# A two-layer graph attention kernel: the sums placed one superchunk behind the links, the merge two behind, the edge features one ahead, with fewer small VectorE instructions

## The chip, the cores and the metric

The kernel runs on one core of one Trainium2 chip. The metric is the device time of one execution in microseconds. Three runs of the kernel before gave 5592.37, 5597.21 and 5601.2 us; the median is 5597.21 us.

Five engines and the DMA queues work side by side, each through its own list of instructions in order, and they wait for each other through semaphores. TensorE (PE) multiplies matrices into PSUM, VectorE (DVE) and ScalarE (ACT) work on tiles in SBUF and PSUM, GpSimd (POOL) here issues the gathers, and SyncE (SP) issues the plain DMAs.

## What is computed

Two graph attention layers over N = 6250 nodes with 256 features and E = 200000 edges that are sorted by destination. Every node also has a loop edge to itself, whose features are the mean over its incoming edges. The outer call is `x + two_layers(relu(layernorm(x)))`. One layer is, with the setup left out:

```python
te = relu(edge_attr @ We + be) * exp(x @ Wo + bo)[src][:, None]
s2, d2, ea2 = _add_self_loops(src, dst, te, n)
hx = (x @ Wg).reshape(n, h, f)
he = (ea2 @ Wge).reshape(-1, h, f)
al = leaky_relu(einsum('nhf,hf->nh', hx, a_s)[s2] + einsum('nhf,hf->nh', hx, a_d)[d2]
                + einsum('ehf,hf->eh', he, a_e), 0.2)
m = segment_max(al, d2, num_segments=n)
al = exp(al - m[d2])
al = al / segment_sum(al, d2, num_segments=n)[d2]
out = segment_sum(hx[s2] * al[:, :, None], d2, num_segments=n) + b
```

Layer 0 has 4 heads of 64 features and a relu behind its residual, layer 1 has one head of 256. All data is float32.

## The kernel before

A prologue makes the table T of layer 0: for each node a row of transformed features and small per-node terms. The edges of a layer are cut into 1563 chunks of 128 edges, one edge to a partition, and the chunks into 66 superchunks: 64 of 24 chunks, then one of 14 and one of 13. A step of the main loop (`edges`) works on one superchunk `st`; the names `nx`, `pv` and `pp` mean the superchunk after it, the one before it and the one before that. The two layers make 132 steps. The instructions are written out by hand in the order in which each engine runs them.

What belongs to one superchunk, with the lines that the profile names:

- `gather` (L769): 24 indirect DMAs on POOL's queue, 128 rows of T each, into one of three buffers G. The gather of superchunk k needs the buffer of superchunk k - 3, so it waits until that one's sums are done. It is issued a step ahead, at the start of the step of k - 1; the sums that it waits for run in the step before that one.
- `nodes` (L823, L825): SP's loads of the destination window's rows (tw). `load_ea`, `load_lb` and `load_fl` load edge attributes, positions and flags for two superchunks at a time.
- `spread` (L859, L861), `parts` (L881 to L893; L890 is a matmul into the PSUM tile zad), `rphase1` (matmuls L842 into y, ACT copies L843 into R), `rphase2` (L851, from R into zad), `adst` (matmuls L907 into zad, transposes L909, a reduction L911): the edge features and the destination's term, as a row for each edge.
- `logits` (L922 to L936, DVE): the attention logits and two scans that give running maxima of each destination's edges within a partition's line of chunks.
- `ends` (L947, L948, PE transposes; L950, ACT): the ends of these lines, turned so that the 128 partitions lie in one row, are copied from the PSUM tile lf into LF.
- `links` (L962 to L969, DVE; L974, PE): two scans over LF and the flags chain the partitions' maxima, and transposes bring the result back into a tile named lf. That PSUM tile has one buffer.
- `maxima` (L984 to L1006): the maxima of each edge's destination, the weights exp(al - m) in kps and the factor pr for what is carried over from the superchunk before.
- `onehots` (L871): the selection matrices S that say which edge belongs to which row of the window.
- `scale` (L1032): the gathered rows in G times their weights, in pieces of 6 chunks.
- `carried` (L1017 to L1023): the row that the superchunk before left open (carry) is added into the first row of G.
- `sums` (L1044): S times G, one product per chunk, all 24 into one PSUM tile u; then ACT copies u to U (L1047). A product of float32 shows as two matmul records. `carry` (L1053, L1055) takes the open row from U.
- `merge` and what follows (L1065 to L1119 in layer 0, to L1145 in layer 1), here called `finish`: the loop edge, the normalisation, the residual and, in layer 0, the next layer's input. `rows1` (L1125, L1127) transposes it, `rows2` multiplies it with the next layer's weights (L378), adds (L382), takes one exponential (L1135) and stores the row of T for layer 1 (L1160). In layer 1 `rows2` stores the output (L1165).

In the step of superchunk k the order is: the gather and the loads of k + 1; logits of k; carried and the first 12 sums of k - 1; spread of k + 1; ends of k; rows1 of k - 2; 6 more sums of k - 1; links and onehots of k; rows2 of k - 2; the last 6 sums of k - 1 with U; maxima of k in turn with parts of k + 1; rphase1 of k + 1; the carry of k - 1; scale of k in turn with the merge of k - 1; rphase2 and adst of k + 1. The last superchunk of a layer has a function of its own (`last`), which also starts the next layer.

Of the kernel before, what the change touches and what calls it, by code (L numbers as in the profile page):

```python
# [31 lines left out]
P = 128  # L32
# [46 lines left out]
class Kernel:  # L79
# [279 lines left out]
    def fixed_rows(self):  # L359
        nc, cp = self.nc, self.cp  # L360
        self.crow = crow = [cp.tile([1, L.W], F32, name=f"crow{L.l}") for L in self.L]
        for t in crow:
            nc.gpsimd.memset(t, 0.0)
# [190 lines left out]
    def edges(self, ctx):  # L554
# [24 lines left out]
        drain(self.parts(steps[0]))  # L579
# [4 lines left out]
        pv = pp = None  # L584
        ahead, rest = 1, None
        for k, st in enumerate(steps):

            if ahead < len(self.groups):
                left = self.groups[ahead][0] - 2 - k
                if rest is None and left <= 2:  # L590
                    gi = self.index_load(ahead, self.xp)
                    rest = self.index_group(ahead, self.xp, gi)
                if rest is not None:
                    for _ in range(7):
                        next(rest, None)
                    if left <= 0:
                        drain(rest)
                        ahead, rest = ahead + 1, None
            nx = steps[k + 1] if k + 1 < len(steps) else None
            self.load_lb(k + 2)  # L600
            if st["s"] + 1 == self.NS:
                self.last(st, pv, nx)
                pv = pp = None
                continue
            self.gather(nx)
            self.nodes(nx)
            drain(self.logits(st))
            n = pv["C"] if pv else 0
            if pv:
                self.carried(pv)  # L610
                self.sums(pv, 0, n // 2)
            self.spread(nx)
            self.ends(st)
            if pp:
                self.rows1(pp)
            if pv:
                self.sums(pv, n // 2, 3 * n // 4)
            self.links(st)
            self.load_fl(k + 1)
            if k != self.NS:  # L620
                self.onehots(st)
            if pp:
                self.rows2(pp)
            if pv:
                self.sums(pv, 3 * n // 4, n)
            weave(self.maxima(st), self.parts(nx))
            if k == self.NS:
                self.onehots(st)
            drain(self.rphase1(nx))
            self.load_ea(k + 2)  # L630
            if pv:
                self.carry(pv)
            weave(self.scale(st), self.finish(pv) if pv else ())
            self.rphase2(nx)
            self.adst(nx)
            if nx["s"] + 1 == self.NS:
                n = st["C"]
                self.carried(st)
                self.sums(st, 0, n // 2)
                if pv:  # L640
                    self.rows1(pv)
                self.sums(st, n // 2, 3 * n // 4)
                if pv:
                    self.rows2(pv)
                    pv = None
                self.sums(st, 3 * n // 4, n)
            pp, pv = pv, st
# [4 lines left out]
    def last(self, st, pv, nx):  # L652
# [27 lines left out]
        n = st["C"]  # L680
        self.sums(st, 0, n - 2)
# [6 lines left out]
        self.sums(st, n - 2, n)  # L688
# [4 lines left out]
        self.rows2(st)  # L693
        if nx:
# [4 lines left out]
            drain(self.parts(nx))  # L699
            self.rphase2(nx)  # L700
            self.adst(nx)
            if early:
                self.added(nx, [(w, self.trow1[q["s"] % 2][:, :self.L[1].TW]) for w, q in ((w0, pv), (w1, st))])
# [112 lines left out]

    def nodes(self, st):
        nc, L, s = self.nc, st["L"], st["s"]
        r = nc.sync.value_load(self.base_i[0:1, 0, s:s + 1], min_val=0, max_val=self.N)
        tw = self.np_.tile([P, self.L[0].TW + D], F32, name="tw", bufs=3)  # L820
# [53 lines left out]
    def parts(self, st):  # L874
# [7 lines left out]
        yield  # L882
        V.tensor_sub(r[:, :H], ad, a3[:, :H, 0])
        yield
        V.tensor_copy(a3[:, :H, 1], r[:, :H])
        yield
        V.tensor_sub(a3[:, :H, 2], r[:, :H], a3[:, :H, 1])
        st["zad"] = z = self.ps_1.tile([P, 1024], F32, name="zad")
        q = z[:, 400:400 + 3 * H]
        self.nc.tensor.matmul(q, st["Q"], a3[:, :H, :].rearrange("p h t -> p (h t)"), start=True, stop=True)  # L890
        yield
        st["aq"] = aq = self.aq[st["k"] % 2]
        V.tensor_tensor(aq[:, :, 4:4 + 3 * H], q.unsqueeze(1).to_broadcast([P, 4, 3 * H]),  # L893
                        self.quad.unsqueeze(2).to_broadcast([P, 4, 3 * H]), op=OP.mult)
        yield

    def adst(self, st):


        nc, L, c = self.nc, st["L"], st["C"]  # L900
        H = L.H
        V = nc.vector
        z, lb = st["zad"], st["lb"]
        st["rt"] = rt = self.wp.tile([P, C, 32], F32, name="rt", bufs=1)
        rv = rt.rearrange("p c j -> p (c j)")
        for w, o in self.halves(st):
            nc.tensor.matmul(z[:, o], st["aq"].rearrange("p k j -> p (k j)"), lb[:, w], start=False, stop=True)  # L907
        for w, o in self.halves(st):
            V.transpose(rv[:, w], z[:, o])  # L909
# [30 lines left out]
    def ends(self, st):  # L940
# [5 lines left out]
        pl = self.ps_1.tile([P, 512], F32, name="lf")  # L946
        nc.tensor.transpose(pl[0:H, 1:P + 1], fv[:, :, c - 1], self.ident)  # L947
        nc.tensor.transpose(pl[0:H, P + 1:2 * P + 1], bv[:, :, 0], self.ident)  # L948
# [3 lines left out]
    def links(self, st):  # L952
# [12 lines left out]
        st["cl"] = cl = self.wp.tile([4, 2, P], F32, name="cl")  # L965
        init = -BIG if prev is None else prev["cl"][:H, 0, P - 1:P]
        V.tensor_tensor_scan(cl[:H, 0, :], fl[:H, 1, :], d1[:H, 0, :], init, op0=OP.add, op1=OP.max)  # L967
        V.memset(cl[:H, 1, P - 1:P], -BIG)
# [4 lines left out]
        for i in range(2):  # L973
            nc.tensor.transpose(pc[:, i * H:(i + 1) * H], cl[:H, i, :], self.ident[0:H, 0:H])  # L974

    def maxima(self, st):
# [9 lines left out]
        for i, pen in enumerate((self.fpen, self.lpen)):  # L986
            V.tensor_tensor(th, pen[:, o:o + c].unsqueeze(1).to_broadcast([P, H, c]),  # L987
# [12 lines left out]
        if st["prev"] is not None:  # L1000
            st["pr"] = pr = self.wp.tile([1, 4], F32, name="pr")
            V.tensor_sub(pr[:, :H], pc[0:1, 0:H], mh[0:1, :, 0])
            yield
# [286 lines left out]
def drain(g):  # L1290
    for _ in g:
        pass
# [91 lines left out]
```

## Time and profile before

The profiled execution took 5582.45 us, 5580.7 us of which is its span, from its first instruction to its last.

| what | value |
|---|---|
| runs, median | 5597.21 us |
| profiled execution; its span | 5582.45 us; 5580.7 us |
| mean granted TensorE clock in the span | 0.756 of full speed |
| steps of layer 0: first gather starts | 199.8 us |
| steps of layer 0: last one counted starts | 2781.2 us |
| steps of layer 1: first gather counted starts | 2995.7 us |
| steps of layer 1: last one counted starts | 5487.3 us |
| one indirect DMA of a gather on POOL | 0.95 us, and 0.30 us to the next |
| one gather of 24 | 29.8 to 30.0 us |
| sums, 12 chunks (24 records) at speed; 6 chunks after idle time | 5.63 us; 4.88 us |
| scale, one piece of 6 chunks | 1.75 us |
| onehots of a superchunk | 3.32 us |

How to read the profile: busy times are per engine, in us; shares are of the span. A line of the timeline has the start in us, the duration, the engine, the line of the kernel, the instruction, its output and inputs with the shape, the number of instructions drawn together, and in brackets the idle time just before and what ended it. "remote" stands where the event that released the wait is not one that the profile can name, "issue" where the engine waited for nothing that is shown. In a windows line the window comes first, then its length, then busy time and count of PE, PEld (weight loads), DVE, ACT and POOL, the granted TensorE clock, the busy share of the DMA engines and their GB/s.

### The profile page before, as it was taken

How to read it: one execution, taken by the hardware profiler on the slowest of the kernel's cores; microseconds unless marked ns; L12 is line 12 of the kernel's file. 1: busy time of each engine (PE TensorE's matmuls, PEld its weight loads, DVE VectorE, ACT ScalarE, POOL GpSimd, SP SyncE). 2: the span in 40 equal slices, each digit the busy share in tenths (PEclk: the TensorE clock that was granted, in tenths of full speed). 3: DMA queues.
4: the chain of work that ended last, by engine and by line, in shares of the span. 5: the costliest groups of instructions: out<-in, count | busy, mean ns of one | idle time of the engine just before them, and what ended most of it. 6: DMA issues, size and time to landing. Idle time of an engine off the chain costs nothing. (4 is left out here: it accounts for less than half of the span.)

```text
span 5580.7 us, 39554 instructions
## 1 busy us (share of the span) xinstructions
PE 2861.8 (51%) x10408; PEld 1925.1 (34%) x10408; DVE 2922.8 (52%) x8141; ACT 687.9 (12%) x1910; POOL 2979.8 (53%) x3155
## 2 busy tenths in 40 slices
PE   6455455555555555555654544445444454444445
PEld 4233333333333333333443323333233232333324
DVE  6555555555555555555654544545454454544546
ACT  4111111111111111111110100101010010101001
POOL 3455555555555554555554555555555555555553
PEclk8677777777777777777777777767777777777777
DMA  6333333333333333333333333333333333333332
GB/s 198 94 102 115 104 100 111 107 98 107 109 104 104 111 104 102 108 105 105 104 106 86 101 105 99 107 101 105 104 96 108 99 107 102 99 109 94 110 100 66
DMA packets 246401, 584.96 MB, mean 105 GB/s; under 512 B 62904, under 2 KB 103310, under 8 KB 246104
## 3 DMA queue, kind: packets, MB, share of 16 engines
q0 software_dynamic: 150144, 422.82, 27.4%
q1 hardware_dynamic: 95610, 158.89, 8.8%
q8 instruction: 85, 1.39, 0.1%
q14 instruction: 146, 1.20, 0.1%
q10 hardware_dynamic: 416, 0.67, 0.0%
HBM read 547.87 MB, written 34.37 MB: 104 GB/s over the span
## 5 line engine op out<-in xcount | busy, mean ns | idle before, releaser
L769 POOL DMA_INDIRECT G<-T,src x3114 | 2963.0, 952 | 2546.6 <-issue 905.2
L1044 PE MATMUL u<-G,S 128*128 128x270 f32 (+1 forms) x6252 | 1775.2, 445 | 3.6 <-ACT pr L1006 2.4
L1044 PEld LDWEIGHTS u<-G,S 128*128 128x128 f32 x6252 | 1389.3, 226 | 311.0 <-ACT pr L1006 2.5
L964 DVE TENSOR_TENSOR d<-LF,fl 4x256 f32<-4x256 f32 (+1 forms) x132 | 54.5, 413 | 1907.8 <-ACT LF L950 1902.1
L974 PE MATMUL lf<-ident,cl 4*128 4x4 f32 (+1 forms) x264 | 64.3, 245 | 1917.5 <-DVE cl L967 1903.2
L1032 DVE TENSOR_TENSOR G<-G,kps 128x1536 f32<-128x1536 f32 (+2 forms) x528 | 907.9, 1727 | 1.2 <-ACT R L843 1.2
L974 PEld LDWEIGHTS lf<-ident,cl 4*128 4x128 f32 (+1 forms) x264 | 45.6, 174 | 1980.5 <-issue 1199.7
L842 PE MATMUL y<-ea,webd 64*128 64x384 f32 (+1 forms) x1056 | 423.3, 526 | 24.9 <-ACT R L843 20.1
L871 DVE TENSOR_TENSOR S<-kps,loc 128x3072 f32<-128x3072 f32 (+2 forms) x133 | 432.8, 3254 | 0.1
L950 ACT ACTIVATE LF<-lf 4x256 f32<-4x256 f32 (+1 forms) x132 | 49.5, 375 | 2992.4 <-remote 2819.5
L947 PE MATMUL lf<-ident,fw 128*4 128x128 f32 (+1 forms) x132 | 41.2, 312 | 568.8 <-issue 263.9
L843 ACT ACTIVATE R<-y,webd 128x384 f32<-128x384 f32 (+2 forms) x528 | 293.2, 568 | 107.0 <-PE y L842 76.1
L842 PEld LDWEIGHTS y<-ea,webd 64*128 64x128 f32 x1056 | 181.7, 193 | 267.9 <-ACT R L843 136.3
L947 PEld LDWEIGHTS lf<-ident,fw 128*4 128x4 f32 (+1 forms) x132 | 10.7, 81 | 619.3 <-issue 522.1
L851 PE MATMUL zad<-R,wea 128*64 128x384 f32 (+1 forms) x1056 | 208.9, 517 | 0.3 <-DVE aq L893 0.3
L909 DVE STREAM_TRANSPOSE rt<-zad 128x384 f32<-128x384 f32 (+1 forms) x264 | 136.0, 553 | 37.8 <-remote 32.9
L1023 DVE TENSOR_TENSOR G<-G,crow 1x270 f32<-1x270 f32 (+1 forms) x130 | 55.8, 429 | 174.6 <-remote 102.8
L378 PE MATMUL fin<-wg,h1T 128*128 128x260 f32 x264 | 134.3, 662 | 4.0 <-ACT h1T L1127 3.6
L859 DVE TENSOR_TENSOR lb<-lb,kps 128x768 bf16<-128x768 bf16 x132 | 122.0, 924 | 11.4 <-issue 11.4
L1047 ACT ACTIVATE U<-u 128x270 f32<-128x270 f32 (+1 forms) x132 | 51.9, 393 | 597.6 <-PE zad L890 534.8
L851 PEld LDWEIGHTS zad<-R,wea 128*64 128x64 f32 x1056 | 66.8, 141 | 126.1 <-issue 108.1
L893 DVE TENSOR_TENSOR aq<-zad,quad 128x48 bf16<-128x48 f32 (+1 forms) x132 | 25.4, 193 | 148.4 <-PE zad L890 147.6
(197 smaller groups left out, 2552.5 us busy)
## 6 DMA issues: line engine op xcount, KB each, us to landing
G<-T,src POOLq DMA_INDIRECT x3114
ea<-in_ea_dram SPq DMA_DIRECT2D x64, 768.0 KB
lb<-locrow SPq DMA_DIRECT2D x64, 384.0 KB
T<-t1row SPq DMA_DIRECT2D x66, 260.0 KB
tw<-T SPq DMA_DIRECT2D x66, 258.0 KB
tw<-T SPq DMA_DIRECT2D x66, 134.0 KB
tw<-in_x_dram SPq DMA_DIRECT2D x66, 128.0 KB
out_dram<-fb SPq DMA_DIRECT2D x64, 128.0 KB
```

What stands on the lines that cost most here:

```text
L378: self.nc.tensor.matmul(ps[:, :L.MW], hT[:, k, :], self.wg[L.l][:, k, :], start=(k == 0), stop=(k == 1))
L769: nc.gpsimd.indirect_dma_start(out=G[:, c, 0:L.TW], out_offset=None, in_=self.rows[L.l][0:n * (1 + L.l), :], in_offset=bass.IndirectOffset ...
L842: nc.tensor.matmul(y[:, :n], self.webd[l][r, :], ea[r, w], start=True, stop=True)
L843: nc.scalar.activation(R[:, i, w], y[:, :n], AF.Relu, bias=self.be[l])
L851: nc.tensor.matmul(st["zad"][i * PH:(i + 1) * PH, o], self.wea[l][0], R[:, i, w], start=True, stop=False)
L859: V.tensor_tensor(lb[:, :n], lb[:, :n], self.k_part.to_broadcast([P, n]), op=OP.is_equal)
L871: nc.vector.tensor_tensor(st["S"][:, c0:c1, :], self.k_iota.unsqueeze(1).to_broadcast(w), self.loc[:, o + c0:o + c1].unsqueeze(2).to_broad ...
L909: V.transpose(rv[:, w], z[:, o])
L974: nc.tensor.transpose(pc[:, i * H:(i + 1) * H], cl[:H, i, :], self.ident[0:H, 0:H])
L1023: V.tensor_add(g, g, cr)
L1032: nc.vector.tensor_tensor(v, v, pw[:, c0:c1, :].unsqueeze(3) .to_broadcast([P, c1 - c0, H, L.F]), op=OP.mult)
L1044: nc.tensor.matmul(u[:, :L.W], S[:, i, :], G[:, i, 0:L.W], start=(j == 0), stop=(j == c - 1))
```

## The change

The step of superchunk k gets another order. After the gather and the loads of k + 1 come rphase1 of k + 1, logits and ends of k, spread and parts of k + 1, carried of k - 1, rows1 of k - 3, links of k, the rest of the edge features' matmuls of k + 1 (`blocks`, rphase2, adst), onehots of k, the matmuls of rows2 of k - 3, all 24 sums of k - 1 in one run, maxima and scale of k, what is left of the rows of k - 3 (`rows3`), the merge of k - 2, the transposes and the reduction of k + 1 (`edge_rows`), the copy U of k - 1 (`evict`) and its carry. Copies and instructions that belong to the index work stand behind that. Four buffers instead of three hold tw, three instead of two hold U. The gather still has three buffers G, and its wait is for the same sums.

Beside this some DVE instructions go: the clearing of an element of cl in each step (done once, in two fixed tiles), one of two transposes where the number of chunks is even, two of four pieces of scale, one instruction of `carried`, and, where there is one head, several of `maxima`, `carried` and `merge`, by forms that do two operations in one instruction. In the built program DVE has 7164 instructions in place of 8143; PE, ACT and POOL have as many as before.

The core of the diff:

```diff
@@ edges
             self.gather(nx)
             self.nodes(nx)
+            drain(self.rphase1(nx))
+            self.load_ea(k + 2)
             drain(self.logits(st))
-            n = pv["C"] if pv else 0
+            self.ends(st)
+            self.spread(nx)
+            self.parts(nx)
             if pv:
                 self.carried(pv)
-                self.sums(pv, 0, n // 2)
-            self.spread(nx)
-            self.ends(st)
-            if pp:
-                self.rows1(pp)
-            if pv:
-                self.sums(pv, n // 2, 3 * n // 4)
+            if pr:
+                self.rows1(pr)
             self.links(st)
             self.load_fl(k + 1)
+            self.blocks(nx)
+            self.rphase2(nx)
+            self.adst(nx)
             if k != self.NS:
                 self.onehots(st)
-            if pp:
-                self.rows2(pp)
+            if pr:
+                self.rows2(pr)
             if pv:
-                self.sums(pv, 3 * n // 4, n)
-            weave(self.maxima(st), self.parts(nx))
+                self.sums(pv)
+            drain(self.maxima(st))
             if k == self.NS:
                 self.onehots(st)
-            drain(self.rphase1(nx))
-            self.load_ea(k + 2)
+            drain(self.scale(st))
+            if pr:
+                self.rows3(pr)
+            if pf:
+                drain(self.finish(pf))
+            self.edge_rows(nx)
...
             if pv:
+                self.evict(pv)
                 self.carry(pv)
-            weave(self.scale(st), self.finish(pv) if pv else ())
-            self.rphase2(nx)
-            self.adst(nx)
+            pr, pf, pv = pf, pv, st
...
@@ nodes
-        tw = self.np_.tile([P, self.L[0].TW + D], F32, name="tw", bufs=3)
+        tw = self.np_.tile([P, self.L[0].TW + D], F32, name="tw", bufs=4)
@@ parts, now without turns; its last instruction is a function of its own
+    def blocks(self, st):
+        H = st["L"].H
         st["aq"] = aq = self.aq[st["k"] % 2]
-        V.tensor_tensor(aq[:, :, 4:4 + 3 * H], q.unsqueeze(1).to_broadcast([P, 4, 3 * H]),
-                        self.quad.unsqueeze(2).to_broadcast([P, 4, 3 * H]), op=OP.mult)
+        self.nc.vector.tensor_tensor(aq[:, :, 4:4 + 3 * H],
+                                     st["zad"][:, 400:400 + 3 * H].unsqueeze(1).to_broadcast([P, 4, 3 * H]),
+                                     self.quad.unsqueeze(2).to_broadcast([P, 4, 3 * H]), op=OP.mult)
@@ adst keeps its matmuls; the rest is edge_rows
+    def edge_rows(self, st):
...
+        if c % 2:
+            for w, o in self.halves(st):
+                V.transpose(rv[:, w], z[:, o])
+        else:
+            V.transpose(rv[:, :32 * c].rearrange("p (b n) -> p b n", b=2),
+                        z.rearrange("p (b n) -> p b n", b=2)[:, :, :16 * c])
@@ ends
+        nc.tensor.transpose(pl[0:H, P + 1:2 * P + 1], bv[:, :, 0], self.ident)
         nc.tensor.transpose(pl[0:H, 1:P + 1], fv[:, :, c - 1], self.ident)
-        nc.tensor.transpose(pl[0:H, P + 1:2 * P + 1], bv[:, :, 0], self.ident)
@@ links
-        st["cl"] = cl = self.wp.tile([4, 2, P], F32, name="cl")
+        st["cl"] = cl = self.cl[st["k"] % 2]
...
-        V.memset(cl[:H, 1, P - 1:P], -BIG)
@@ maxima
         for i, pen in enumerate((self.fpen, self.lpen)):
+            if H == 1:
+                V.scalar_tensor_tensor(m[:, :n], pen[:, o:o + c], pc[:, i:i + 1], m[:, :n], op0=OP.add, op1=OP.max)
+                yield
+                continue
@@ carried
+            if H == 1:
+                V.scalar_tensor_tensor(g[:, :D + 1], cv[0:1, :D + 1], pr[:, 0:1], g[:, :D + 1], op0=OP.mult, op1=OP.add)
...
-    def scale(self, st, piece=6):
+    def scale(self, st, piece=12):
@@ sums
-    def sums(self, st, c0, c1):
+    def sums(self, st):
...
-        if c0 == 0:
-            st["u"] = self.ps_1.tile([P, 512], F32, name="u")
-        u = st["u"]
-        for j in range(c0, c1):
+        st["u"] = u = self.ps_1.tile([P, 512], F32, name="u")
+        for j in range(c):
             i = (j + 1) % c
             nc.tensor.matmul(u[:, :L.W], S[:, i, :], G[:, i, 0:L.W], start=(j == 0), stop=(j == c - 1))
-        if c1 == c:
-            st["U"] = U = self.np_.tile([P, 272], F32, name="U")
-            nc.scalar.activation(U[:, :L.W], u[:, :L.W], AF.Copy)
+
+    def evict(self, st):
+        L = st["L"]
+        st["U"] = U = self.np_.tile([P, 272], F32, name="U", bufs=3)
+        self.nc.scalar.activation(U[:, :L.W], st["u"][:, :L.W], AF.Copy)
```

`last` and the end of a layer follow the same order, with `sums`, `evict`, `rows3`, `blocks` and `edge_rows` in their places.

## What the change was predicted to do

> **What bounds the kernel now.** I read the table of engines first.
>
> ```profile
> PE 2861.8 (51%) x10408; PEld 1925.1 (34%) x10408; DVE 2922.8 (52%) x8141; ACT 687.9 (12%) x1910; POOL 2979.8 (53%) x3155
> ```
>
> Nobody is full, so the time is in waits. The view of waits, costliest first (engine, tile, line <- what ended the wait: total us, times, longest):
>
> ```profile
> ACT LF L950 <- remote: 2819.5, 120, 25.9
> PE lf L974 <- DVE cl L967: 1903.2, 125, 19.9
> DVE d L964 <- ACT LF L950: 1902.1, 123, 19.9
> ...
> POOL G L769 <- ACT U L1047: 726.4, 58, 13.5
> POOL G L769 <- ACT kps L994: 675.3, 60, 12.7
> ```
>
> Three engines wait for one copy, LF (L950), in nearly every one of 132 steps, and afterwards POOL waits to start the next gather. The timeline of one layer-0 step shows the order:
>
> ```profile
> 2020.63 0.94 POOL L769 DMA_INDIRECT G<-T,src  x1 [12.27 <-ACT U L1047]
> ...
> 2025.42 5.63 PE L1044 MATMUL u<-G,S 128*128 128x270 f32 x24
> ...
> 2040.47 0.37 PE L948 MATMUL lf<-ident,bw 128*4 128x128 f32 x1 [0.24 <-DVE crow L1021]
> ...
> 2041.07 4.88 PE L1044 MATMUL u<-G,S 128*128 128x270 f32 x12
> ...
> 2049.46 0.94 POOL L769 DMA_INDIRECT G<-T,src  x1 [0.30 <-issue]
> 2054.58 0.38 ACT L950 ACTIVATE LF<-lf 4x256 f32<-4x256 f32 x1 [19.73 <-remote]
> ...
> 2063.18 0.40 ACT L1047 ACTIVATE U<-u 128x270 f32<-128x270 f32 x1 [3.11 <-PE zad L890]
> ```
>
> The gather runs from 2020.63 to 2050.4 (24 x 1.25 = 30 us). L948, LF's only late operand, ends by its record at 2040.84; LF starts at 2054.58, 13.7 us later and 4 us after the gather. In 124 of 128 full steps LF starts 3.3 to 4.2 us after the end of the gather, whenever L948 ended. The trace's semaphore records say why: late in a gather TensorE's completions come out singly, 4 to 6 us apart (here 2032.66, 2036.93, 2041.13, 2046.03, 2051.63), and eleven leave together at 2054.44 to 2054.85. L948's stands behind the sums' (L1044), each of the first 18 of 24 of which signals. So a step is gather 30 us, flush 4, then links, last sums and U: 8.3 us in layer 0, 7.2 in layer 1, until the buffer is free.
>
> Five steps escaped. One of them, in layer 1:
>
> ```profile
> 3651.32 0.94 POOL L769 DMA_INDIRECT G<-T,src  x1 [11.30 <-ACT kps L994]
> ...
> 3664.15 0.38 ACT L950 ACTIVATE LF<-lf 1x256 f32<-1x256 f32 x1 [4.88 <-issue]
> ...
> 3685.73 0.18 DVE L987 TENSOR_TENSOR mt<-fpen,lf 128x24 f32<-128x24 bf16 x1 [15.14 <-remote]
> 3686.59 0.94 POOL L769 DMA_INDIRECT G<-T,src  x1 [4.40 <-ACT U L1047]
> ```
>
> Here LF came 13 us into the gather, links and sums ran under it, and the next gather began 4.4 us after the end of this one. The five last 35.0, 36.5, 35.0, 35.3, 34.9 us: mean 35.3.
>
> **The sum's base.** The windows view over the two runs of steps (first column the window, then its length):
>
> ```profile
> 199.80:2781.20 2581.40, 1403.78 (x4823) 939.05 (x4823) 1432.62 (x3832) 340.79 (x961) 1395.34 (x1465) 0.76 0.36 105
> 2995.70:5487.30 2491.60, 1159.55 (x4455) 778.47 (x4455) 1196.01 (x3296) 245.09 (x673) 1387.79 (x1464) 0.75 0.36 103
> ```
>
> That is 62 intervals of 41.6 us and 61 of 40.85: 5073.0 us, 41.24 each. The other 507.7 us of the 5580.7 us span are the prologue, the turn between layers and the end. The median of the runs, 5597.21, lies 16.5 us above the span; I add that at the end.
>
> **Part 1: the sums move.** In each step 12 sums left PE ahead of the ends' transposes (L947, L948) and 6 more ahead of the links' (L974). All 24 now stand after links, rphase2, adst and rows2, as one run with one signal. In the built program PE's signals fall from 4165 to 1650, those of the sums from 2433 to 182, a steady step's from about 31 to 12.5. Gone ahead of L950: 12 signals and 5.6 us of matmuls. The new order on PE after a gather starts: U 0.4, the carry 0.6 + 0.4 (L1053, L1055), y (L842) 8 records of 0.53, with ACT's four R copies ahead of LF on its queue, the ends 0.7, a hop of 0.5 or so: 7 us. The logits run beside it on VectorE from the gather's start, 2.3 us, since the edge features are ready; where VectorE is late by its 24 us of work a step, 2 more. So LF lands 6 to 9 us into the gather; PE's signals there still come 0.5 to 2 us apart. Then d and two scans (0.41 + 0.47 + 0.41), L974 0.5, L851 1.5, L907 0.5, in layer 0 L378 2.1, and the sums: 24 records take 5.63 us warm and 12 cold ones 4.88, so 48 take 11.3 to 13.3. They end some 21 us (layer 1, warm) to 29 us (layer 0, late and cold) into the gather. Their one signal is what the next gather waits for (the buffer of two steps back). A lone late signal took 4 to 6 us, or left at the flush: bounded by nothing, a step of 30 us, and by the flush plus U, the short steps' 4.4 to 5.0 us. I take the short step, 35.3 us, nearest in kind: 123 x 35.3 = 4342, against 5073, a saving of 731.
>
> **Part 2: edge features ahead, merge behind.** rphase1 (L842, L843), rphase2, adst and L909, L911 change places within the step, the same instructions. The old cover of rphase1 was the start of the gather too. aq (now the L908 multiply) stands on DVE behind links and ahead of onehots and maxima: if its matmul's signal is late, these wait, then scale, and logits of the next step. The merge's store and LF's table rows go out one step later, on an SP queue that carries a handful of issues per step; DMA is at a 0.36 share. load_ea is issued at the gather's start, as before. All at 0; uncovered, L842 to L911 cost 4.2 + 1.5 + 0.5 + 1.0 + 0.5 = 7.7 us a step. onehots (L871, 3.3 us) comes to lie inside the gather; in the short steps it did, and the gather took 30.2 against 29.8 to 30.0 us: at most 0.4 x 123 = 49 us, and then less gap.
>
> **Part 3: fewer VectorE instructions.** 8143 become 7164. At 0.16 to 0.31 us for such hops, about 0.2, 979 of them are 196 us, 1.6 a step. VectorE works 23.6 of 43.3 us and 19.8 of 40.6 in the steps looked at: cover is enough, so 0; all on the path, 196 us. scale in two pieces is 2 x 3.5 for 4 x 1.75: 0, bounded by one piece's start, 0.2 us.
>
> Sum: 507.7 + 4342 = 4850 of span, 4866 as a median. The 507.7 keep their work; I give them plus or minus 20.
>
> **A rule against this reading.** The Trainium skill, SBUF — State Buffer, section Who interferes with whom, says that a DMA never contends with a compute engine. By it no signal would be held because a gather runs, and the sum would be the first rival's. The rows of LF, tied to the end of the gather in 124 of 128 steps, differ, and they decide.
>
> **Rivals.**
> *POOL sets the step.* If the sums' signal passes in the gather, the next gather follows at once: 30 us a step, 507.7 + 123 x 30 = 4198, as a median 4214. For: the sums end 1 to 9 us before the gather does. Against: the prologue's 60 gathers without a gap, where PE's signals came up to 26.6 us apart; without gaps nothing flushes.
> *Half the gain.* Maxima need L974's signal. In the short step above they started only 34.4 us in (L987), with scale, merge and L909 behind, about 14 us: logits of the next step are late, and LF lands 15 us into that gather, where a part sticks. A short step and an old one in turn, 35.3 and 41.24: 38.3 a step, 5215, as a median 5231; with fewer short ones up to no change.
> *Slower.* The change puts everything behind one signal. Where LF still misses its window it comes 34 us in, as now; but then the whole PE queue follows it: LF 0.4, scans 1.3, 0.5 + 1.5 + 0.5 + 2.1, 11.3 to 13.3 of sums, U 0.4 and about 1 of hops: 19 to 21 us in place of 8.3, a step of 53 to 55, in layer 1 some 51 to 53. In that long gap signals are prompt, so the next step is short: 35.3 and 53 in turn, 44.15 a step, 5938, as a median 5955. All steps held: 7027. It decides from a mean step of 41.24 us, one held step in three. For: the late maxima of the short steps, and VectorE's hops of 4.5 us (L1023, waiting for L1021) 18 to 20 us into a gather. Against: those stood with 18 sums' signals pending, which are gone; in the prologue, with PE idle, VectorE's hops were prompt 23 us in.
>
> **How the numbers follow.** Short steps nearly throughout (33 to 38 us): 0.45. POOL-bound: 0.09. Half the gain: 0.11, of it 0.02 within 0.2% (about what this measurement can tell from no change). Slower: 0.35. So faster 0.63, same 0.02, slower 0.35. The likeliest one's own range is 33 us (4567) to 38 (5182), as medians 4583 to 5198. For 8 in 10 I go down to 32 us a step with the rest 20 lower, 4440, leaving POOL-bound out, and up to 6050, a little beyond the alternating case, leaving out some 0.1 of the slower ones.
>
> **What would show it.** Right: LF starts 5 to 10 us after its gather starts; the sums are one group of 48 records ending before the gather does; L769's wait is 4 to 5 us and ends with U (now L1077); the waits for LF fall from 2819.5 to some hundreds. POOL at 85% of the span and waits for L769 near 0 would show the first rival. Gaps in turn of 5 and over 20 us, with LF 4 us after the gather in every second step, the slower one. The prediction is wrong if completions are held with few pending as they are with many.

## The result, and the profile after

The changed kernel took 5067.05 us (median of 4 runs, 5066.21 to 5067.33), the kernel before 5599.2 us in the same comparison (5592.37 to 5610.43): a ratio of 0.9048, 95% interval 0.9032 to 0.9063. The profiled execution's span is 5065.5 us. The sum forecast 4850 of span, so the direction and most of the size are there, and 215 us of the gain are not.

First the table of engines of the changed kernel, and its view of waits (engine, tile, line <- what ended the wait: total us, times, longest):

```profile
PE 3205.6 (63%) x10408; PEld 1925.9 (38%) x10408; DVE 2930.4 (58%) x7162; ACT 712.1 (14%) x1910; POOL 2983.0 (59%) x3155
```

```profile
ACT U L1077 <- PE u L1072: 1372.4, 113, 17.0
PE u L1072 <- issue: 1226.2, 667, 4.3
POOL G L779 <- ACT U L1077: 944.9, 123, 49.5
...
DVE d L985 <- ACT LF L971: 364.8, 101, 19.8
```

The 2819.5 us that ACT waited for LF are gone from the top; the first place now belongs to U, the copy of the sums. New is the second line: TensorE waits 1226.2 us inside the sums, 667 times, for nothing that the profile can name. In the profile before, waits of this kind inside the sums were 1.2 us in all. VectorE is as busy as before (2930.4 against 2922.8 us) with 979 instructions fewer; the 196 us that the prediction worked out for them did not come off it.

The windows view of the two runs of steps (window, length, busy times and counts, granted TensorE clock, DMA share, GB/s):

```profile
215.70:2541.40 2325.70, 1493.88 (x4815) 892.48 (x4813) 1459.78 (x3587) 352.93 (x958) 1393.09 (x1464) 0.73 0.42 117
2765.90:4983.30 2217.40, 1409.59 (x4454) 827.11 (x4453) 1176.84 (x2625) 255.51 (x671) 1394.45 (x1465) 0.70 0.42 115
```

Each is 61 intervals: 38.1 us in layer 0, 36.4 in layer 1. (The prediction counted 62 in layer 0, one too many; one gather there has a gap of 2.1 us in its middle. The old step in layer 0 is 42.3 us, and the sum with 122 intervals would have been 4814.) The rest of the span is 522.4 us against 507.7.

One step of layer 0 in the timeline, rows of POOL, ACT and PE in order of time:

```profile
1167.43 0.94 POOL L779 DMA_INDIRECT G<-T,src  x1 [7.24 <-ACT U L1077]
...
1173.99 0.37 ACT L971 ACTIVATE LF<-lf 4x256 f32<-4x256 f32 x1
...
1181.05 6.54 PE L1072 MATMUL u<-G,S 128*128 128x270 f32 x28
1187.88 0.39 PE L1072 MATMUL u<-G,S 128*128 128x270 f32 x1 [0.29 <-issue]
1189.99 0.39 PE L1072 MATMUL u<-G,S 128*128 128x270 f32 x1 [1.72 <-issue]
1192.81 0.61 PE L1072 MATMUL u<-G,S 128*128 128x270 f32 x1 [2.44 <-issue]
1194.22 0.61 PE L1072 MATMUL u<-G,S 128*128 128x270 f32 x1 [0.80 <-issue]
1199.11 0.61 PE L1072 MATMUL u<-G,S 128*128 128x270 f32 x1 [4.29 <-issue]
1201.21 5.31 PE L1072 MATMUL u<-G,S 128*128 128x270 f32 x15 [1.49 <-issue]
...
1206.56 0.40 ACT L1077 ACTIVATE U<-u 128x270 f32<-128x270 f32 x1 [7.01 <-PE u L1072]
...
1207.29 0.94 POOL L779 DMA_INDIRECT G<-T,src  x1 [10.16 <-ACT U L1077]
```

LF comes 6.6 us into the gather. Then 28 of the 48 records of the sums run in 6.5 us, the next five take 13 us, and the last 15 run at once from 1201.21, 4.1 us after the gather's last indirect DMA ended at 1197.1. So the flush is still there. It no longer holds LF; it holds the tail of the sums, and with it U and the next gather: 10.2 us of gap in this step, mostly 6 to 11 in layer 0 and 5 to 8 in layer 1, where the short steps of before had 4.4 to 5.0.

### The profile page after: what moved, and what is told of

It reads as the page before. It is cut to its first block, busy times and chain, and to the rows that moved or that the text cites. A ratio compares the mean times of both kernels' runs of the same rounds, so it can differ in the third digit from the quotient of the medians.

```text
span 5065.5 us, 37717 instructions
## 1 busy us (share of the span) xinstructions
PE 3205.6 (63%) x10408; PEld 1925.9 (38%) x10408; DVE 2930.4 (58%) x7162; ACT 712.1 (14%) x1910; POOL 2983.0 (59%) x3155
## 5 line engine op out<-in xcount | busy, mean ns | idle before, releaser
L1072 PE MATMUL u<-G,S 128*128 128x270 f32 (+1 forms) x6252 | 1821.2, 435 | 1288.8 <-issue 1226.2
L1072 PEld LDWEIGHTS u<-G,S 128*128 128x128 f32 x6252 | 1331.7, 214 | 1723.3 <-issue 1413.1
L1062 DVE TENSOR_TENSOR G<-G,kps 128x3072 f32<-128x3072 f32 (+1 forms) x270 | 863.0, 3239 | 8.8 <-issue 1.8
L857 PE MATMUL y<-ea,webd 64*128 64x384 f32 (+1 forms) x1056 | 561.3, 704 | 47.3 <-issue 29.8
L943 DVE TENSOR_TENSOR G<-rt,G 128x96 f32<-128x96 f32 (+1 forms) x132 | 30.2, 229 | 629.3 <-DMA G<-T,src 616.7
L857 PEld LDWEIGHTS y<-ea,webd 64*128 64x128 f32 x1056 | 237.8, 255 | 344.9 <-issue 177.3
L866 PE MATMUL zad<-R,wea 128*64 128x384 f32 (+1 forms) x1056 | 351.9, 817 | 0.3 <-DVE aq L908 0.3
L1083 PE MATMUL fin<-U,lsel 128*1 128x270 f32 (+1 forms) x260 | 112.0, 525 | 150.0 <-ACT U L1077 150.0
L929 DVE STREAM_TRANSPOSE rt<-zad 128x768 f32<-128x768 f32 (+1 forms) x130 | 126.2, 971 | 32.0 <-remote 28.4
L994 PEld LDWEIGHTS lf<-ident,cl 4*128 4x128 f32 (+1 forms) x264 | 34.2, 180 | 268.4 <-issue 258.2
L1044 DVE SCALAR_TENSOR_TENSOR G<-carry,pr,G 1x257 f32<-1x257 f32 x65 | 32.7, 502 | 164.8 <-ACT carry L1085 164.8
L1083 PEld LDWEIGHTS fin<-U,lsel 128*1 128x1 f32 x260 | 11.1, 81 | 252.4 <-ACT U L1077 252.4
L915 PE MATMUL zad<-lb,aq 128*128 128x384 bf16 (+1 forms) x264 | 97.3, 468 | 0.0
```

The costliest lines, as they stand in the source:

```text
L857: nc.tensor.matmul(y[:, :n], self.webd[l][r, :], ea[r, w], start=True, stop=True)
L866: nc.tensor.matmul(st["zad"][i * PH:(i + 1) * PH, o], self.wea[l][0], R[:, i, w], start=True, stop=False)
L915: self.nc.tensor.matmul(st["zad"][:, o], st["aq"].rearrange("p k j -> p (k j)"), st["lb"][:, w], start=False, stop=True)
L929: V.transpose(rv[:, :32 * c].rearrange("p (b n) -> p b n", b=2), z.rearrange("p (b n) -> p b n", b=2)[:, :, :16 * c])
L1062: nc.vector.tensor_tensor(v, v, pw[:, c0:c1, :].unsqueeze(3) .to_broadcast([P, c1 - c0, H, L.F]), op=OP.mult)
L1072: nc.tensor.matmul(u[:, :L.W], S[:, i, :], G[:, i, 0:L.W], start=(j == 0), stop=(j == c - 1))
```

## The experiments

Something came out that no single pair of kernels could show. The runs were made in five groups, each with the kernel before beside it on the same chip. In two groups the kernel before took 4077.8 and 4076.45 us, in three 5618.31, 5584.52 and 5584.64 us, and within a group all runs of all kernels were of one kind. One chip showed both. I call the second kind "held", since the traces of the first have none of the held completions described above. The measurement of the result was held. What sets it was not found.

The records of semaphore signals differ as well. In the trace of the changed kernel above, 1223 of TensorE's 1650 signals have a record, 3283 of VectorE's 5876 and 1031 of ScalarE's 1872; in the run of the same kernel that was not held, none is missing. So it is not TensorE alone that is touched. Whether the recording of the trace has itself a part in the hold was not tested.

**The shorter VectorE forms alone, in the old order.** Of the change only these forms, without the larger pieces of scale. The core of the edit:

```diff
-        st["cl"] = cl = self.wp.tile([4, 2, P], F32, name="cl")
+        st["cl"] = cl = self.cl[st["k"] % 2]
-        V.memset(cl[:H, 1, P - 1:P], -BIG)
...
+            if H == 1:
+                V.scalar_tensor_tensor(m[:, :n], pen[:, o:o + c], pc[:, i:i + 1], m[:, :n], op0=OP.add, op1=OP.max)
```

> The kernel before in its old order, with only the shorter VectorE forms of the change (fixed cl tiles, one transpose for two, the one-head forms): 595 VectorE instructions fewer, scale still in 4 pieces. Theory that the time is in what TensorE gives out late while a gather runs: VectorE's work is covered, the steps stay at 41.2 us, the ratio lies between 0.994 and 1.003. Rival, that the small VectorE instructions are on the path: 595 x 0.2 us = 119 us, a ratio of 0.979.

Measured, not held: 4075.08 us against 4077.8, ratio 0.9992 (0.9983 to 1.0001). By the profile it has 721 VectorE instructions fewer (7420 against 8141), not 595. VectorE's small instructions are covered there. Under the hold this was not run, so there the rival stays undecided.

**The move of the sums alone, in the old order.**

```diff
                 self.carried(pv)
-                self.sums(pv, 0, n // 2)
...
-                self.sums(pv, n // 2, 3 * n // 4)
...
-                self.sums(pv, 3 * n // 4, n)
+                self.sums(pv, 0, n)
```

> The kernel before with only the place of the sums changed: all 24 in one run behind links and rows2, the edge features and the merge where they were. Theory A, that only signals are held and that few signals ahead of LF are enough: LF comes during the gather in nearly every step, the steps fall to 36 to 39 us, ratio 0.89 to 0.95. Theory B, that TensorE retires all its instructions in order, with or without a signal, through a queue of about 64, and in the later part of a gather only one per 0.7 to 2.1 us: LF comes earlier, but the logits stand 14 us into the gather, so the 96 instructions of the sums begin late, most of them after the gather's flush: 30 + 4 + 6 to 10 us, 40 to 44 a step, ratio 0.98 to 1.06.

Measured, not held: 4415.22 us, ratio 1.0825 (1.0809 to 1.0842). Both theories spoke of held completions, so it separates nothing between them. It shows that the move, without a hold, costs: the steps of layer 0 are 34.2 us, their gathers some 4 to 5 us apart. Under the hold the move alone was not run.

**The changed kernel with the sums directly behind links.**

```diff
             self.links(st)
             self.load_fl(k + 1)
+            if pv:
+                self.sums(pv)
             self.blocks(nx)
...
-            if pv:
-                self.sums(pv)
             drain(self.maxima(st))
```

> The changed kernel with the 24 sums directly behind links; the matmuls of blocks, rphase2, adst and rows2 (24 to 32 TensorE instructions a step, weight loads counted) come behind them. Theory B (queue of about 64, slow retirement late in the gather): that many instructions fewer stand ahead of the end of the sums, each worth 0.5 to 1.2 us, so the gap between gathers shrinks from 5 to 11 us to 4 or 5: steps of 34.5 to 35.5 us, 4770 to 4900 us, ratio to the kernel before 0.85 to 0.875. Theory A (only signals held): the sums start 4 us earlier, but U still leaves at the flush: 36 to 37 us a step, ratio 0.895 to 0.91.

Measured, not held: 4254.61 us, ratio 1.0426 (1.041 to 1.0442). Again not under the hold, so it was run once more below.

**Half of the sums' products.**

```diff
-        for j in range(c):
+        for j in range(0, c, 2):
...
-        self.nc.scalar.activation(U[:, :L.W], st["u"][:, :L.W], AF.Copy)
+        self.nc.scalar.activation(U[:, :L.W], st["u"][:, :L.W], AF.Copy, bias=1.0)
```

> The changed kernel with every second product of the sums left out (12 of 24 chunks; 1.0 is added to U so that nothing is divided by zero), so 48 TensorE instructions a step fewer. Theory B: all instructions of a step are in the queue early, and the sums' last one retires before or near the gather's end: gaps of 0 to 3 us, steps of 30 to 33 us, 4200 to 4580 us. Rival, that U always waits for the flush 4 us after a gather's end: gaps of 4.4 to 5 us, 35.3 a step, about 4860 us.

One run, not held: 4113.85 us against 4077.8. With nothing held it tells only that the steps (30.4 and 30.3 us) are POOL's.

**The changed kernel itself, unedited.**

> The changed kernel itself, unedited, because in the last runs the kernel before took 4077.8 us with its gathers back to back, not 5599. Theory: the change saves only the time that TensorE's held completions cost. Where the kernel before takes about 4078 us (nothing held), the changed one has nothing to save and its longer serial chain (links, 28 more TensorE matmuls, all sums, U) shows: 4200 to 4420 us, ratio 1.03 to 1.085, as the two kernels with moved sums had (1.043 and 1.083). Where the kernel before takes about 5600 us, the ratio is 0.905 again. Rival, that the change saves work or waits of its own: faster than the kernel before in both.

Measured, not held: 4137.73 us against 4076.45, ratio 1.0153 (1.0136 to 1.017): 1.5% slower, clear of the interval, though less than the 2% below which two kernels count as the same here. The theory's direction held, its size (1.03 to 1.085) was too large. The windows view of its two runs of steps (61 and 60 intervals), and one stretch of its timeline:

```profile
167.30:2026.30 1859.00, 1326.67 (x4823) 830.13 (x4821) 1450.05 (x3575) 360.67 (x963) 1412.73 (x1465) 0.78 0.52 146
2207.90:4024.50 1816.60, 1156.80 (x4390) 739.25 (x4388) 1149.02 (x2568) 259.03 (x665) 1377.72 (x1440) 0.78 0.50 139
```

```profile
1003.18 11.10 PE L1072 MATMUL u<-G,S 128*128 128x270 f32 x48
...
1017.49 0.38 ACT L1077 ACTIVATE U<-u 128x270 f32<-128x270 f32 x1
```

That is 30.5 and 30.3 us a step, the gathers back to back, and all 48 records of the sums in one run of 11.1 us while a gather runs. The old order with the shorter forms, in the other group of this kind, has 30.2 and 30.1. So POOL sets the step in both kernels. Of the 69.7 us between these two spans, 4133.3 and 4063.6, the steps give 26.5, the turn between the layers (181.6 against 151.3 us) 30.3, and the prologue and the end the rest.

**The changed kernel with the sums ahead of links.**

```diff
             if pv:
                 self.carried(pv)
+                self.sums(pv)
             if pr:
                 self.rows1(pr)
...
-            if pv:
-                self.sums(pv)
             drain(self.maxima(st))
```

> The changed kernel with all 24 sums ahead of links (directly behind the ends and carried), the rest of the change kept. If nothing is held (kernel before at 4078 us): the sums end some 7 us earlier and the buffer is free before the gather ends, so POOL sets the step, 30 us: 4060 to 4120 us, ratio 0.995 to 1.01. If completions are held (kernel before at 5600 us): LF still comes early, but links' transposes stand behind 96 sums instructions and come out at the flush, maxima and scale after it: 36 to 42 us a step, 4950 to 5700 us, ratio 0.885 to 1.02.

Measured, not held: 4480.52 us, ratio 1.0997 (1.0978 to 1.1015). I was wrong by 400 us. From its view of waits:

```profile
PEld fin L1082 <- ACT U L1076: 1275.1, 130, 15.2
...
ACT kps L1017 <- DVE mt L1015: 1008.6, 130, 15.7
```

In layer 1 the sums do end earlier, 18 us into the gather (median) where the changed kernel without a hold has 22, and the step is 30.2 us. In layer 0 they end later, 34 us where it has 25. U stands on ACT behind the weights of maxima and the merge's copies, and these now wait for links behind the sums. The carry waits for U, y for the carry's place on PE, LF for y: a loop of 35.6 us in layer 0. It is a chain through queues, without any hold.

**The old order with all 24 sums in one run ahead of the ends.**

```diff
                 self.carried(pv)
-                self.sums(pv, 0, n // 2)
+                self.sums(pv, 0, n)
...
-                self.sums(pv, n // 2, 3 * n // 4)
...
-                self.sums(pv, 3 * n // 4, n)
```

> The kernel before with all 24 sums in one run directly behind carried, ahead of the ends, instead of 12, 6 and 6; nothing else changed. Only chunk 0, which comes last, needs carried, so the sums can start 5 us into the gather. If completions are held (kernel before at 5600 us): U and LF leave together at the flush, the next gather follows 4.4 to 5 us after the end of the last one, links and maxima run under it: 35 to 36 us a step, 4830 to 4950 us, ratio 0.865 to 0.885. If nothing is held (kernel before at 4077 us): POOL sets the step in both, 4060 to 4100 us, ratio 0.995 to 1.006. A rival for both: the ends behind 96 more instructions cost what the sums gain, ratio 1.02 or more.

Measured, held: 5444.41 us against 5618.31, ratio 0.9697 (0.9677 to 0.9718), 40.8 and 39.7 us a step. Not the 35 to 36 expected: in layer 0 LF, now behind all the sums, comes 10 us after the end of the gather (median). The reason is the most exact thing these runs show. TensorE's semaphore records and issues of one step, with the number of the instruction counted from the gather's start (weight loads and matmuls both count; which record belongs to which instruction follows from counting back from the 16 at the end, since earlier ones are missing):

```
410.74 ... 420.84   #34 to #110 issue, 0.2 us apart in the sums
421.81, 423.21, 424.61   three issues: #113, #114, #116
426.00   completion of #54        426.01   #117 issues
431.60   completion of #58        431.61   #121 issues
433.02 to 433.66   16 completions, 0.04 us apart; #123 and all after it issue freely
```

At 426.00 and at 431.60 the instruction that issues is the 63rd behind the one that completes. In the step of the changed kernel shown above, the last matmul of L379 completes at 1193.51 (VectorE's L383, which waits for it, starts at 1193.53), and the weight load that starts then is again the 63rd behind it. So in these three places TensorE runs on for 63 instructions without completions. Here the completions come at 1.4 us an instruction (four in 5.6 us), and the next instruction waits, whether it signals or not. 24 chunks are 96 instructions, and 28 of them, #123 to #150, were left for the flush.

**The changed kernel with the sums directly behind links and U ahead of the merge.** The sums' move is the edit shown above; the rest is

```diff
...
             drain(self.scale(st))
+            if pv:
+                self.evict(pv)
             if pr:
                 self.rows3(pr)
+            if pv:
+                self.carry(pv)
             if pf:
                 drain(self.finish(pf))
...
-            if pv:
-                self.evict(pv)
-                self.carry(pv)
```

> The changed kernel with the sums directly behind links, as before, and now also the copy U directly behind scale and the carry behind rows3, ahead of the merge, so that U no longer stands behind the merge's copies on ScalarE. If nothing is held: layer 0's step falls from the 32.4 us of the kernel that only had the sums first to POOL's 30 us: 4070 to 4140 us, ratio 0.998 to 1.016. If completions are held: 34.5 to 36 us a step, 4770 to 4960 us, ratio 0.85 to 0.885.

Measured, held: 5201.49 us, ratio 0.9243 (0.9212 to 0.9274). Layer 1 is as expected, 35.8 us a step, though U, which waits for the flush, now stands ahead of the merge's exponential on ACT (`DVE mg L1112` waits 680 us for it there). Layer 0 is not: short and long steps in turn, 40.2 us on average. VectorE's view of the timeline in the maxima of a step whose gather began at 336.0 us:

```profile
363.07 0.26 DVE L1015 TENSOR_TENSOR m<-m,mt 128x96 f32<-128x96 f32 x1 [3.31 <-remote]
364.47 0.26 DVE L1012 TENSOR_TENSOR mt<-lpen,lf 128x96 f32<-128x96 bf16 x1 [1.14 <-DVE m L1015]
365.87 0.26 DVE L1015 TENSOR_TENSOR m<-m,mt 128x96 f32<-128x96 f32 x1 [1.14 <-DVE mt L1012]
367.27 0.26 DVE L1017 TENSOR_TENSOR mt<-al,m 128x96 f32<-128x96 f32 x1 [1.14 <-DVE m L1015]
```

Instructions that wait for the one before them on their own engine start 1.4 us apart, twice 0.7, where they take 0.26. In the two runs without a hold that have maxima as late as 20 to 25 us into a gather (the sums moved alone, and the sums directly behind links), the second L1012 and the L1015 behind it start at most 0.39 us apart. So under the hold VectorE's chains of small steps late in a gather are slow too; scale, merge and the next logits then come late, and LF of the next step comes 21 us into its gather. Which of the two moves brought maxima into that window was not separated here.

**The sums directly behind links, again.**

> The kernel with only the sums moved directly behind links, unedited, because it has only been seen where nothing was held (ratio 1.043). Where completions are held: the window of about 63 TensorE instructions fills with sums and not with 28 others, so fewer of the sums are left for the flush. The variant with U first had steps of 35 to 36.5 us in layer 1, and lost in layer 0 only through U standing ahead of the merge on ScalarE. So 35 to 37.5 us a step in both layers, 4830 to 5130 us, ratio 0.865 to 0.915, against 0.905 of the change. Rival, that maxima and scale, or rows2 behind the sums, then come late and the next step's LF with them: over 0.925.

Measured, held: 5068.9 us against 5584.52, ratio 0.9078 (0.9062 to 0.9095): 38.8 us a step in layer 0, 35.3 in layer 1. Layer 1 gains 1.1 us a step on the change, layer 0 loses 0.7, and as a whole it is no better. From its view of waits:

```profile
DVE rt L929 <- PE zad L915: 824.0, 61, 15.4
```

The edge features' last matmul now stands behind the sums, comes out with them at the flush, and VectorE cannot make the next step's rows before: what stands behind the sums comes late, as the rival said, though it named maxima, scale and rows2, and at a part of its price.

**A pause in POOL's queue.** The test of what holds the completions.

```diff
...
         for c in range(c0, st["C"]):
+            if c == C // 2 and c0 == 0:
+                for _ in range(12):
+                    nc.gpsimd.memset(self.scratch, 0.0)
             nc.gpsimd.indirect_dma_start(
```

> The changed kernel with twelve memsets of a scratch tile (about 0.55 us each, 6.5 us in all) on POOL's queue between the 12th and the 13th indirect DMA of each gather. Where completions are held (kernel before at 5600 us): if what holds them is the running gather, TensorE's completions flush some 4 us into the pause, 19 us after the gather's start, the sums run freely after it and end under the second half, and the next gather follows 0 to 3 us after the end of this one: 36.5 to 39.5 us a step, 5010 to 5380 us, ratio 0.895 to 0.96, although POOL's queue has 6.5 us more in each step. Rival, that the hold ends only with the whole gather: 36.5 + 7 to 9, 44 to 46 us a step, 5930 to 6180 us, ratio 1.06 to 1.10. Where nothing is held (kernel before at 4077 us) POOL sets the step and the pause is paid in full: 4137 + 128 x 6.5 = 4970 us, ratio 1.22.

Measured, held: 5043.3 us against 5584.52, ratio 0.9034 (0.9019 to 0.9049). POOL does about 835 us more (its busy time is 3817.5 us against 2983.0), and the time is not longer. Rows of its timeline:

```profile
876.47 11.10 PE L1076 MATMUL u<-G,S 128*128 128x270 f32 x48
877.77 6.95 POOL L782 MEMSET scratch<- 128x512 f32 x12
884.87 0.95 POOL L783 DMA_INDIRECT G<-T,src  x1 [0.15 <-issue]
892.63 0.38 ACT L1081 ACTIVATE U<-u 128x270 f32<-128x270 f32 x1
```

The sums run through in 11.1 us, as without a hold; completions of matmuls ahead of them are recorded at 881.30 and 881.37, 3.5 us into the pause. Over the whole run TensorE waits 38.4 us inside the sums for nothing that the profile can name, where the changed kernel had 1226.2. In most steps the next gather follows the second half directly, and the step is 37.5 and 37.0 us, which is 30 us of gather and 7.1 of pause: POOL sets it again. The hold ends when the indirect DMAs pause, not with the whole gather.

**A shorter pause.** Eight memsets, 4.8 us.

> The changed kernel with eight memsets in place of twelve between the 12th and the 13th indirect DMA, so that POOL's queue pauses for 4.7 us and not 7.1. Where completions are held: the flush came 3.5 us after the last indirect DMA of the first half, so 4.7 us are still enough, and POOL sets the step: 34.8 us against 37.2 with the long pause; 123 steps x 2.4 = 295 us less than its 5043: 4750, with some steps that miss the flush up to 4900 us, ratio 0.85 to 0.878. Rival, that the pause must be longer than the flush of 63 instructions and the sums behind it: 5050 to 5300 us. Where nothing is held the pause is paid: 4137 + 128 x 4.7 = 4740 us, ratio 1.16.

Measured, held: 4787.99 us against 5584.64, ratio 0.8585 (0.8563 to 0.8607), 35.8 and 34.7 us a step. This is the fastest version run under the hold. Where nothing is held it was not run; I estimate 4137 + 128 x 4.8 = 4750 us there, since POOL sets the step.

**The pause alone, in the old order.** The same twelve memsets in the kernel before.

> The kernel before, in its old order with 12, 6 and 6 sums and all its VectorE instructions, with only the twelve memsets between the 12th and the 13th indirect DMA of each gather. Where completions are held: if the time was in completions that the running gather holds, the flush in the pause lets the sums' and the ends' completions out, LF comes 20 to 24 us after the gather's start, and POOL sets the step, 37.2 us in place of 41.24: 507.7 + 123 x 37.2 = 5083, so 5040 to 5200 us, ratio 0.90 to 0.93, as much as the whole change. Rival, that the order of the work was the cause and the pause only adds: 5600 to 6400 us, ratio 1.0 to 1.15. Where nothing is held: 4077 + 128 x 7.1 = 4986 us, ratio 1.22.

Measured, held: 5047.73 us against 5584.64, ratio 0.9035 (0.9018 to 0.9053), 37.9 and 37.0 us a step:

```profile
1029.01 6.95 POOL L772 MEMSET scratch<- 128x512 f32 x12
1032.54 0.27 PE L951 MATMUL lf<-ident,fw 128*4 128x128 f32 x1 [3.09 <-DVE fw L938]
...
1033.01 0.38 ACT L954 ACTIVATE LF<-lf 4x256 f32<-4x256 f32 x1 [6.53 <-PE lf L952]
```

Nine completions of TensorE are recorded 0.04 us apart from 1031.04, 2.0 us into the pause, and LF starts 4.0 us into it; the median over the steps is 22 us into the gather, some 7 us after the pause began. The old order, with every signal and every VectorE instruction it had, gains by this one edit what the whole change gained.

## Why the prediction came out as it did

**What bounds the kernel: right, with one word wrong.** LF bound nearly every step, and it was tied to the gather's end: in 116 of the 122 steps counted (the prediction's 124 of 128 does not come out of the trace) it starts 3.3 to 4.2 us after it. That a running gather is what holds it, the pause shows: the old kernel with nothing but a pause is at 0.9035. But it is not signals that stand in line. In the three places counted, an instruction issues when the 63rd before it completes, signal or not; late in a gather that is one per 0.7 to 2.8 us, and signals are only where it can be seen. The prediction's own condition for being wrong, "if completions are held with few pending as they are with many", came true in part: with 12.5 signals a step they were held just the same.

**The sums' move: right for LF, mis-sized for the sums.** LF was put 6 to 9 us into the gather; it comes after 4 to 7. That the sums ahead of it had held it fits the run with all 24 sums ahead of the ends, where LF comes 10 us after the gather; but the move alone was not run under the hold, so its share of the 0.9048 is argued from the timeline. The term that failed is "They end some 21 us (layer 1, warm) to 29 us (layer 0, late and cold) into the gather", taken from matmuls at full rate. The window of 63 stops them at the 15th chunk in the step shown, and in most steps they end 4 to 10 us after the gather (median 7.3 in layer 0, 6.0 in layer 1). The step was put at the short steps' 35.3 us, which in the old order had needed only the tail of 6 sums; measured are 38.1 and 36.4. That is 201 us of the 215, and the other 15 are the rest outside the steps, which was given plus or minus 20. The step's own error is larger, and luck hid part of it: the sum counted one interval too many, 35 us; over the 122 there are, the steps take 237 us more than 35.3 us each.

**VectorE's instructions: right at nothing, where it was tried**, 0.9992 for 721 of the 979 without a hold, where POOL sets the step. Under the hold it is only seen that VectorE is as busy as before.

**The edge features and the merge at nothing: not shown.** None of the runs moved them alone. Their matmuls now stand ahead of the sums and take places in the window; with the sums ahead of them the step of layer 1 is 1.1 us shorter and that of layer 0 0.7 us longer. Without the hold the turn between the layers costs 30 us more; the prediction did not look there.

**The rivals.** POOL's step, priced at 30 us and 4214, is what the kernel has where nothing is held: 4137, but the old one then has 4077, and the rival said nothing of that. Half the gain has a step of 38.3 us, close to the 38.1 of layer 0, but not its way there: LF was not late. The slower rival, LF held and everything behind it, did not come: LF passed in all full steps. Slower by another way, the longer chain without a hold, did come in the runs of that kind, and no rival had it. So the direction, too, owes something to luck: the measurement fell where completions are held, as the profile before had, and nothing in the prediction knew of the other condition. Its range, 4440 to 6050 us, took in everything from a fifth less to a loss.

**The rule of the Trainium skill** (SBUF — State Buffer, section Who interferes with whom, that a DMA never contends with a compute engine) fits the runs that were not held, with 48 records in 11.1 us beside a gather. It does not fit the held ones, where a pause of the indirect DMAs set TensorE free 3.5 us later. The section speaks of ports of SBUF, and no run here tells whether these have a part in it.

Two things stay open: what sets whether a group of runs is held, and what in the gather holds the engines, its descriptors, its data, its semaphores, or what it does to the recording of the trace. No run told these apart.

## What to carry to other kernels

When an engine's instructions start late with nothing to wait for, count how many it has in flight: here 63 TensorE instructions, weight loads counted, and what matters is how many stand ahead of the one that others need. A queue that is not full can still be in the way: giving POOL some 840 us more to do (3821.9 us busy against 2979.8) took 9.7% off the old kernel, so test a suspected hold by a pause before reordering the work. And run the kernel before beside every variant: the change is worth 0.905 in one condition and 1.015 in the other, and only the pair tells which one a number belongs to.

## What was not expected of the hardware

- The same kernel took 4077 or 5585 us, by group of runs, on one and the same chip, with a spread below 0.4% inside each group.
- TensorE's window of 63 instructions between issue and completion, seen three times, and instructions of the sums issuing 0.7, 1.4, 2.1 or 2.8 us apart, a grid of 0.7 us, while indirect DMAs run in the held step shown.
- After the last indirect DMA the completions flush within 1.8 to 4.5 us (median 3.8 to 3.9 us in the old order, with a pause and without), 0.04 us apart, in the middle of a gather as well as at its end.
- In held runs more than signals of TensorE come late: VectorE's small steps start up to 2.1 us apart late in a gather, and many semaphore records of all three compute engines are missing.
